# Layer 1's probabilities turned by VectorE's blocks and a way by DRAM, and dequantisation's comparisons as rectified differences on ScalarE

## The chip, the cores and the metric

The kernel runs on one core of one Trainium2 chip. A core has five engines that the text names as the profile does: PE (TensorE, the matrix products; PEld is its weight load), DVE (VectorE), ACT (ScalarE), POOL (GpSimd) and SP (SyncE, which issues most DMAs). Data lies in SBUF (128 partitions), products go to PSUM, and inputs, outputs and scratch lie in DRAM. The metric is the device time of one execution in microseconds.

## The reference

Four pairs of an attention and a feed-forward part (layers 0 to 3) work on `x` of 8 x 128 x 512 and a context of the same shape; each adds its result to `x`, which is normalised in front of it. All of it is fp32. Two places matter here. Layer 1's attention takes each batch's 128 x 512 matrix as four windows of 128 columns, and in each window has 8 heads of 8 channels:

```python
qh = q.reshape(BN, H, dh, W)          # BN = 8 batches x 4 windows, H = 8, dh = 8, W = 128
kh = k.reshape(BN, H, dh, W)
vh = val.reshape(BN, H, dh, W)
scores = jnp.einsum('bhdi,bhdj->bhij', qh, kh) / jnp.sqrt(jnp.asarray(dh, qh.dtype))
scores = jnp.where(mp[:, :, None, :] > 0, scores, jnp.asarray(-1000000000.0, scores.dtype))
attn = jax.nn.softmax(scores, axis=-1)
o = jnp.einsum('bhij,bhdj->bhdi', attn, vh).reshape(BN, DK, W)
```

Layer 2's feed-forward weights are first rounded to 16 levels per block of 64 (NF4), with the block's largest magnitude as its scale:

```python
normalized = flat / jnp.where(absmax == 0, 1.0, absmax)
bounds = (NF4_CODE[:-1] + NF4_CODE[1:]) * 0.5
idx = jnp.searchsorted(bounds, normalized)
return (NF4_CODE[idx] * absmax).reshape(shape)
```

Three matrices of 1376 x 512 go through this.

## The kernel before, in words

**Units.** Layers 0 and 2's attention are 128 units, each one head of 128 channels for four batches ("half"): units 0 to 31 and 32 to 63 are Layer 0's two halves, 64 to 95 and 96 to 127 Layer 2's. A unit projects keys, queries and (per group of four heads) values, makes scores (L265), takes the softmax (reduction L256 and reciprocal L259 on DVE, exponentials L213 on ACT), turns the probabilities, weighs the values (L288), and after each fourth head projects to the output (L218). Step `u` of the main loop projects for unit `u+3`, scores unit `u+2` and weighs unit `u`, so a unit's probabilities have two steps in which to be turned. Turning goes by `turn_far`: DVE transposes 32 x 32 blocks (L277), SP sends the tile to a DRAM scratch `far` and reads it back in four DMAs in which the blocks change places. Only the first three units turn by PE (`turn`).

**Side work.** Between the pieces of a unit the main loop calls `slot()`. A table gives for each slot what else runs there: while Layer 0's second half runs, the table holds Layer 0's feed-forward, Layer 1 and its feed-forward for the first half's four batches (`short_stages`); the same for the second half stands beside Layer 2's first half. The side work has a stream of its own (`side`), with three PSUM buffers for all purposes; the units' stream (`main`) has two for projections and one each for transposes, scores and weighed values.

**Layer 1.** Per batch and window `n`, `score` (slot t+2+3n) makes the 8 heads' scores with two products (L532), adds the mask, takes the softmax over 128 x 8 x 128 in one tile `s` (L534, L536, L213, L539, L540). `turn` (slot t+7+3n) transposes the 8 heads on PE (L225, two groups of four into PSUM) and copies each group to SBUF on ACT (L228). `weigh` (slot t+9+3n) multiplies with the values (L551, 8 products of 32 columns).

**Dequantisation.** The three weight matrices pass in 34 chunks of up to 128 x 512. In each, `nf4_round` takes 15 steps: a comparison of the weights with a bound, times the difference of two levels (L725; the first, L721, writes the sum itself), and an addition to the sum (L726), both on DVE. The steps are generated one at a time, and each `slot()` lets through as many as `NF4_PACE` says for the stage (a pair per half: with the table still filled, and after). Each chunk is then transposed on PE and written to DRAM for Layer 2's feed-forward.

**What sets the order.** The program is recorded as above; a scheduler in the framework then orders each engine's instructions, and each engine runs its own list in order, waiting on semaphores. SP's list holds the weight loads, whose 20 buffers are freed by PE, and the trips by DRAM, in one queue; a DMA that reads what another has written waits on SP for it. Layer 3 follows the units; it makes the same trip by DRAM through its method `far`, at 128 x 768 for queries and keys and 128 x 1024 for probabilities.

Of the kernel before, what the change touches and what calls it, by code (L numbers as in the profile page):

```python
# [62 lines left out]
def kernel(ctx: ExitStack, tc: tile.TileContext, a, out):  # L63
# [157 lines left out]
    def p_transposed(st, p, engine=None):  # L221
# [8 lines left out]
            V.tensor_copy(pt, tp)  # L230
        return pt

    def project(st, w, xT):

        mm = st.mm()
        for c in range(DC):
            T.matmul(mm, lhsT=w[:, c, :], rhs=xT[:, c, :], start=c == 0, stop=c == DC - 1)  # L237
        return mm

    def tile_of(name, bufs, shape=(P, 512)):  # L240
        return qkv.tile(list(shape), F32, tag=name, name=name, bufs=bufs)
# [6 lines left out]
    class Unit:  # L248
# [24 lines left out]
            self.pt = [pt[:, i, :] for i in range(HALF)]  # L273

        def turn_far(self):
            tb = tile_of("tb", 1, (P, 4, HALF, 32))
            V.transpose(tb, self.p.rearrange("p i (c k) -> p c i k", k=32))  # L277
            far = dram.tile([4, 32, 4, P], F32, tag="far0", name="far0", bufs=4)
            load(far.rearrange("a k b n -> (a k) (b n)"), tb.rearrange("p c i j -> p (c i j)"))
            pt = self.st.wide("pt", (P, 4, HALF, 32))  # L280
            for b in range(4):
                load(pt[32 * b:32 * b + 32].rearrange("p a i j -> p a (i j)"), far[:, :, b, :].rearrange("a k n -> k a n"))
            self.pt = [pt[:, :, i, :] for i in range(HALF)]

        def weigh(self):
# [28 lines left out]

    def l0_rms(st, h):

        sq = st.wide("sq", bufs=1)
        ss = st.small(1, "ss")
        S.activation(sq, h, AF.Square, accum_out=ss)
        V.tensor_scalar(ss, ss, 1.0 / D, 1e-5, ALU.mult, ALU.add)  # L320
        done = inv_sqrt(ss, [P, 1])
        r = st.wide("pt", (P, 4, P)).rearrange("p c q -> p (c q)")
        V.tensor_scalar(r, h, ss, None, ALU.mult)
        return r, done

# [144 lines left out]
    class L1:  # L470
        def __init__(self, st, hf):
            self.st, self.hf = st, hf
            self.pools = ExitStack()
            self.l1 = self.pools.enter_context(tc.tile_pool(name="l1", bufs=2))
            l1c = self.pools.enter_context(tc.tile_pool(name="l1c", bufs=1))
            self.wqk = l1c.tile([P, 3, 64], F32, name="wqk")
            load(self.wqk, a["l1_wqkv"])
            self.wo = l1c.tile([P, P], F32, name="wo1")
            G.memset(self.wo, 0.0)
            for h in range(8):  # L480
                r = 32 * (h % 4) + 8 * (h // 4)
# [12 lines left out]
            self.vt = l1c.tile([P, 4, 8, 32], F32, name="vt")  # L494
            G.memset(self.vt, 0.0)
            self.s, self.pts = {}, {}

        def norm(self, b):
            mk = self.l1.tile([P, D], F32, tag="mk", name="mk", bufs=1)
            load(mk, a["mask_ff1"][b].to_broadcast([P, D]))  # L500
            self.neg = self.l1.tile([P, D], BF16, tag="neg", name="neg", bufs=1)
            V.tensor_scalar(self.neg, mk, 0.0, -BIG, ALU.is_le, ALU.mult)
            self.ct = load_ctx(self.st, b)
            self.h = layernorm(self.st, b)
# [20 lines left out]

        def score(self, b, n):
            st, w = self.st, slice(n * P, (n + 1) * P)
            s = self.s[n] = self.l1.tile([P, 8, P], F32, tag="s1", name="s1")
            scs = [st.sc() for j in range(2)]
            for j in range(2):  # L530
                r = slice(32 * j, 32 * (j + 1))
                T.matmul(scs[j], lhsT=self.qk[r, w], rhs=self.km[r, :, w], start=True, stop=True)  # L532
            for j in range(2):
                V.scalar_tensor_tensor(s[:, 4 * j:4 * j + 4, :], scs[j], 1.0 / math.sqrt(8.0), times(self.neg[:, w], 4), ALU.mult, ALU.add)  # L534
            mx = st.small(8, "mx")
            V.tensor_reduce(mx, s, AX.X, ALU.max, negate=True)  # L536
            su = st.small(8, "su8")
            exps(lambda h: s[:, h, :], lambda h: s[:, h, :], su, 8, mx)
            V.reciprocal(su, su)  # L539
            V.tensor_mul(s, s, along(su, P))  # L540

        def turn(self, b, n):
            self.pts[n] = [p_transposed(self.st, self.s[n][:, 4 * j:4 * j + 4, :], S) for j in range(2)]

        def weigh(self, b, n):
            if n == 0:
                self.o = self.l1.tile([P, D], F32, tag="o1", name="o1", bufs=1)
            pv = self.st.pv()
            for j in range(2):
                for i in range(4):  # L550
                    T.matmul(pv[32 * i:32 * i + 32, 0, :], lhsT=self.vt[:, n, 4 * j + i, :], rhs=self.pts[n][j][:, i, :], start=j == 0, stop=j == 1)  # L551
            S.copy(self.o[:, n * P:(n + 1) * P], pv[:, 0, :])

        def close(self, b):
            self.y = self.st.wide("sq", bufs=1)
            load(self.y, a["mask_ff1"][b].to_broadcast([P, D]))
            S.activation(self.o, self.o, AF.Gelu)

# [7 lines left out]
    class F1:  # L566
# [33 lines left out]
        def output(self, b):  # L600
            mm = self.st.mm()
            for c in range(DC):
                T.matmul(mm, lhsT=self.qt[b][:, c, :], rhs=self.wb16[:, c, :], start=c == 0, stop=c == DC - 1)
            y = self.st.wide("sq", bufs=1)
# [109 lines left out]

    def nf4_round(dst, w):

        for i, (cmp, bound, step) in enumerate(NF4_STEPS):
            if i == 0:  # L720
                V.tensor_scalar(dst, w, bound, step, cmp, ALU.mult)  # L721
                continue
            ind = nfp.tile([P, 512], F32, tag="ind", name="ind", bufs=1)
            iv = ind[:w.shape[0], :w.shape[1]]
            V.tensor_scalar(iv, w, bound, step, cmp, ALU.mult)  # L725
            V.tensor_add(dst, dst, iv)  # L726
            yield

    def nf4_scales(ri, am):

# [169 lines left out]
    class L3:  # L900
# [50 lines left out]
            V.tensor_scalar(it.rq, it.rq, P * 1e-6, None, ALU.add)  # L951
            inv_sqrt(it.rq, [P, 4])

        def far(self, src, h, tag):

            n = src.shape[2] // P
            tb = self.l3.tile([P, 4 * n, h, 32], F32, tag="tb" + tag, name="tb3", bufs=1)  # L960
            V.transpose(tb, src.rearrange("p h (c k) -> p c h k", k=32))
            far = dram.tile([4, 32, n, 4, 32 * h], F32, tag="far" + tag, name="far", bufs=4)
            load(far.rearrange("a i s b n -> (a i) (s b n)"), tb.rearrange("p c h j -> p (c h j)"))
            pt = self.l3.tile([P, n, 4, h, 32], F32, tag="pt" + tag, name="pt3", bufs=3)
            for b in range(4):
                load(pt[32 * b:32 * b + 32].rearrange("p s a h j -> p s a (h j)"), far[:, :, :, b, :].rearrange("a i s n -> i s a n"))
            return pt

        def turn(self, it):
            it.t = self.far(it.qk, 6, "qk")[:, 0]  # L970

        def order(self, it):

# [4 lines left out]
            it.kT = t[:, :, 4:6, :].rearrange("p a s j -> p s a j")  # L978

        def turn_near(self, it):  # L980
            t = self.l3.tile([P, 6, P], F32, tag="ptqk", name="pt3", bufs=3)
            for h in range(0, 6, 2):
                tp = self.st.tp()[:, 0:2, :]
                for j in range(2):
# [25 lines left out]
            it.pts = [p_transposed(self.st, it.p[:, :, j * P:(j + 1) * P]) for j in range(2)]  # L1010

        def turn_blocks(self, it):
            pt = self.far(it.p, 4, "p")
            it.pts = [pt[:, j].rearrange("p a h j -> p (a h j)") for j in range(2)]

        def weigh(self, it):
# [76 lines left out]
    with ExitStack() as early:  # L1093
# [3 lines left out]
        ps = sub_pool("ps", 1, space=PSUM)  # L1097
        qkv = sub_pool("qkv", 5)
        nfp = sub_pool("nf4", 2)
        main = Stream("m", sub_pool("main", 2), ps, {"mm": ("mm", 2), "tp": ("tp", 1), "sc": ("sc", 1), "pv": ("pv", 1)})  # L1100
        side = Stream("s", sub_pool("side", 2), ps, {k: ("side", 3) for k in ("mm", "tp", "sc", "pv", "po")})


        NF4_PACE = ((2.1, 2.1), (1.0, 2.2), (0.45, 1.2), (1.2, 1.2))
        xT0, xT2 = [], []


# [49 lines left out]
        def short_stages(hf):  # L1157
# [26 lines left out]
            for i, b in enumerate(batches(hf)):  # L1184
                t = 18 + 13 * i
                for n in range(4):
                    call(t + 7 + 3 * n, "l1", "turn", b, n)
                    call(t + 9 + 3 * n, "l1", "weigh", b, n)
                call(t + 18, "l1", "close", b)
                call(t + 19, "l1", "output", b)  # L1190
# [280 lines left out]
```

## Time and profile before

| what | us |
|---|---|
| median of 3 runs (lowest to highest) | 3104.28 (3103.65 to 3104.73) |
| the profiled execution's own time | 3106.4 |
| its span, first to last instruction | 3104.6 |
| mean granted TensorE clock | 0.998 of full |
| DMA: share of 16 engines' span, queue of SP | 36.6% |
| Layer 1's transposes on PE with the first three units' (L225) | 35.3 busy, 268 instructions |
| their copies on ACT (L228) | 35.8 busy, 67 instructions |
| dequantisation's comparisons on DVE (L725, L721) | 210.5 and, of full size, 13.6 |
| dequantisation's additions on DVE (L726) | 326.8 |

A group's row reads: line, engine, operation, written tile <- read tiles, sizes, count, then busy us and mean ns of one, then the idle time of the engine before it and what ended it. PE shows an fp32 product as two instructions, a transpose as one. Matmuls are pipelined, so the length of one overlaps the next; the distance from start to start is what a product takes of PE.

### The profile page before, as it was taken

What the parts mean: (1) busy time and instruction counts of PE and PEld (TensorE: products, weight loads), DVE (VectorE), ACT (ScalarE), POOL (GpSimd) and SP (SyncE); (2) the same over time, 40 slices, a digit from 0 to 9 for tenths busy, and PEclk for the clock granted to TensorE, in tenths of its full rate; (3) what the DMA queues carried; (4) which work ended last, traced back from release to release, by engine and by line L of the source; (5) the groups of instructions that cost most, each with busy time, mean ns of one, the idle gap of its engine ahead of it and who ended that gap; (6) DMA issues with size and microseconds to landing.
All of it is one profiled execution on the core that took longest, in us unless ns stands there. A gap on an engine that the chain in (4) does not pass through costs nothing.

```text
span 3104.6 us, 34843 instructions
## 1 busy us (share of the span) xinstructions
PE 3071.9 (99%) x10976; PEld 1694.2 (55%) x10980; DVE 2015.8 (65%) x4209; ACT 1086.1 (35%) x3410; POOL 295.5 (10%) x315
## 2 busy tenths in 40 slices
PE   9999999999999999999999999999999999999999
PEld 4554555545554565555555554445665665555564
DVE  5877787667767766888989983113555555555544
ACT  3222222235543233655333332002434433333332
POOL 2000000000001021111111110001111111111110
PEclk9999999999999999999999999999999999999999
DMA  6434343333334432323444342223655655555540
GB/s 216 124 113 126 117 126 116 102 103 97 102 95 118 150 119 80 102 82 113 123 140 128 119 124 84 77 69 103 181 178 165 187 180 174 180 172 167 174 132 14
DMA packets 414807, 393.83 MB, mean 127 GB/s; under 512 B 37600, under 2 KB 312736, under 8 KB 414112
## 3 DMA queue, kind: packets, MB, share of 16 engines
q1 hardware_dynamic: 391200, 348.60, 36.6%
q10 hardware_dynamic: 23040, 41.95, 4.4%
q8 instruction: 89, 1.46, 0.2%
q0 software_dynamic: 384, 1.05, 0.1%
q14 instruction: 94, 0.77, 0.1%
HBM read 291.92 MB, written 99.55 MB: 126 GB/s over the span
## 4 chain that ended last, share of the span: by engine, by line
PE 84%; DVE 11%; ACT 2%; DMA 2%; issue 1%; POOL 0%; SPq 0%; ACTq 0%; POOLq 0%; DVEq 0%
PE mm L237 17%; PE mm L218 12%; PE po L218 7%; PE tp L921 7%; PE mm L376 7%; PE mm L944 7%; PE mm L879 5%; PE pv L1019 4%; PE sc L996 3%; PE pv L288 2%; PE mm L888 2%; PE sc L265 2%; ACT s L213 1%; DVE dq L726 1%; DVE rot L656 1%; PE mm L666 1%
## 5 line engine op out<-in xcount | busy, mean ns | idle before, releaser
L237 PE MATMUL mm<-xT,w 128*128 128x512 f32 x1024 | 464.4, 595 | 2.1 <-DVE rot L656 2.1
L218 PE MATMUL mm<-w,o 128*128 128x512 f32 x1024 | 464.0, 597 | 1.6 <-ACT o L290 1.5
L726 DVE TENSOR_TENSOR dq<-dq,ind 128x512 f32<-128x512 f32 (+2 forms) x476 | 326.8, 687 | 9.8
L237 PEld LDWEIGHTS mm<-xT,w 128*128 128x128 f32 x1024 | 188.9, 190 | 218.6 <-issue 208.6
L218 PEld LDWEIGHTS mm<-w,o 128*128 128x128 f32 x1024 | 188.5, 191 | 214.3 <-issue 199.9
L213 ACT ACTIVATE s<-s,nm 128x128 f32<-128x128 f32 x512 | 199.0, 390 | 190.2 <-DVE nm L256 179.1
L944 PE MATMUL mm<-w,xT 128*128 128x512 f32 x512 | 233.9, 592 | 0.0
L218 PE MATMUL po<-w,o 128*128 128x512 f32 x512 | 233.2, 594 | 0.0
L237 PE MATMUL mm<-ctxT,w 128*128 128x512 f32 x512 | 230.7, 593 | 1.1 <-ACT ctxT L1235 0.8
L376 PE MATMUL mm<-w,ctxT 128*128 128x512 f32 x512 | 230.4, 593 | 0.0
L725 DVE TENSOR_SCALAR ind<-nw 128x512 f32<-128x512 f32 (+2 forms) x476 | 210.5, 442 | 5.8
L213 ACT ACTIVATE p<-sc,nm,rq 128x256 f32<-128x256 f32 x256 | 141.1, 562 | 113.6 <-DVE nm L1001 109.9
L159 POOL TENSOR_TENSOR rs<-rs,mhalf 128x1 f32<-128x1 f32 x64 | 41.2, 645 | 1248.5 <-DVE rs L180 757.7
L265 PEld LDWEIGHTS sc<-k,q 128*128 128x128 f32 x1024 | 131.8, 192 | 49.5 <-issue 39.9
L219 DVE TENSOR_TENSOR x<-x,mm 128x512 f32<-128x512 f32 x128 | 87.0, 679 | 110.3 <-PE mm L218 110.0
L290 ACT COPY o<-pv 128x512 f32<-128x512 f32 x128 | 74.3, 581 | 237.6 <-PE pv L288 237.6
L218 PEld LDWEIGHTS po<-w,o 128*128 128x128 f32 x512 | 96.3, 190 | 110.6 <-issue 103.3
L879 PE MATMUL mm<-xT,w 128*128 128x512 f32 (+1 forms) x352 | 152.5, 592 | 0.8 <-DVE x L219 0.8
L376 PEld LDWEIGHTS mm<-w,ctxT 128*128 128x128 f32 x512 | 94.3, 190 | 106.2 <-issue 106.2
L1000 DVE TENSOR_REDUCE nm<-sc 128x2 f32<-128x512 f32 x128 | 85.3, 674 | 102.7 <-PE sc L996 102.5
L237 PEld LDWEIGHTS mm<-ctxT,w 128*128 128x128 f32 x512 | 93.2, 190 | 99.3 <-issue 96.8
L944 PEld LDWEIGHTS mm<-w,xT 128*128 128x128 f32 x512 | 97.0, 190 | 89.5 <-issue 84.9
(244 smaller groups left out, 4716.5 us busy)
## 6 DMA issues: line engine op xcount, KB each, us to landing
w<-in_l_wq SPq DMA_DIRECT2D x128, 256.0 KB
w<-in_l_wo SPq DMA_DIRECT2D x128, 256.0 KB
far<-tb SPq DMA_DIRECT2D x125, 256.0 KB
pt<-far SPq DMA_DIRECT2D x500, 64.0 KB
far<-tb SPq DMA_DIRECT2D x60, 512.0 KB
pt<-far SPq DMA_DIRECT2D x240, 128.0 KB
far<-tb SPq DMA_DIRECT2D x63, 384.0 KB
pt<-far SPq DMA_DIRECT2D x252, 96.0 KB
```

What stands on the lines that cost most here:

```text
L213: S.activation(dst(h), src(h), AF.Exp, bias=negm[:, h:h + 1], scale=by, accum_out=su[:, h:h + 1])
L218: T.matmul(mm, lhsT=o(h), rhs=wo[h], start=h == 0, stop=h == 3)
L237: T.matmul(mm, lhsT=w[:, c, :], rhs=xT[:, c, :], start=c == 0, stop=c == DC - 1)
L265: T.matmul(sc[:, i, :], lhsT=self.q[:, i * P:(i + 1) * P], rhs=k[:, i * P:(i + 1) * P], start=True, stop=True)
L376: T.matmul(mm, lhsT=ctxT[:, c, toks(self.hf * HALF + i)], rhs=grp.wv[c], start=c == 0, stop=c == DC - 1)
L725: V.tensor_scalar(iv, w, bound, step, cmp, ALU.mult)
L726: V.tensor_add(dst, dst, iv)
L879: T.matmul(mm[:n, :], lhsT=w[c][:, j * P:j * P + n], rhs=xT[:, c, :], start=c == 0, stop=c == DC - 1)
L921: T.matmul(it.kv[:, s, :], lhsT=lhsT, rhs=it.wkv[c // 2][:, c % 2, :], start=c == 0, stop=c == DC - 1)
L944: T.matmul(mq, lhsT=self.xT[it.hf][:, c, cols(it.b)], rhs=it.wq[c], start=c == 0, stop=c == DC - 1)
L996: T.matmul(sc[:, i, :], lhsT=it.qT[2 * j + i], rhs=it.kT, start=True, stop=True)
L1019: T.matmul(pv, lhsT=it.v[:, j, :], rhs=it.pts[j], start=j == 0, stop=j == 1)
```

## The change

- Layer 1's `turn` on PE, its PSUM tiles and its copies are gone. At the end of `score`, the 8 heads' probabilities (128 x 1024) are transposed in blocks on DVE, sent to DRAM and read back in four DMAs by a new function `blocks_turned`, which Layer 0's, Layer 2's and Layer 3's trips now use too, with the same layout as before. `weigh` reads the heads' columns as four runs of 32. The tile `s` has one buffer instead of two.
- `nf4_round` no longer compares. ACT makes `max(0, (w - bound) * 2^100)`, which is 0 below the bound and at least the step above it; DVE then takes the minimum with the step and adds it to the sum in one instruction. Downward bounds have the sign turned, with the neighbouring float as bound. ACT works one step ahead; the difference's tile `ind` has two buffers instead of one. A column of 15 constants `bounds` is set on POOL at the start.
- `NF4_PACE` changes for the second to fourth half.
- Some tiles share buffers: the `main` stream's wide tiles come from the tags `o` and `pt0`, the side stream's `sq` has two buffers and also serves for Layer 1's mask and for the first normalisation's result.

```diff
+    def blocks_turned(pool_, src, name, bufs):
+        h, n = src.shape[1], src.shape[2] // P
+        tb = pool_.tile([P, 4 * n, h, 32], F32, tag="tb" + name, name="tb", bufs=bufs[0])
+        V.transpose(tb, src.rearrange("p h (c k) -> p c h k", k=32))
+        far = dram.tile([4, 32, n, 4, 32 * h], F32, tag="far" + name, name="far", bufs=4)
+        load(far.rearrange("a i s b n -> (a i) (s b n)"), tb.rearrange("p c h j -> p (c h j)"))
+        pt = pool_.tile([P, n, 4, h, 32], F32, tag="pt" + name, name="pt", bufs=bufs[1])
+        for b in range(4):
+            load(pt[32 * b:32 * b + 32].rearrange("p s a h j -> p s a (h j)"), far[:, :, :, b, :].rearrange("a i s n -> i s a n"))
+        return pt
...
         def turn_far(self):
...
+            pt = blocks_turned(qkv, self.p, "0", (1, 2))[:, 0]
             self.pt = [pt[:, :, i, :] for i in range(HALF)]
...
         def score(self, b, n):
-            s = self.s[n] = self.l1.tile([P, 8, P], F32, tag="s1", name="s1")
+            s = self.l1.tile([P, 8, P], F32, tag="s1", name="s1", bufs=1)
...
             V.tensor_mul(s, s, along(su, P))
-
-        def turn(self, b, n):
-            self.pts[n] = [p_transposed(self.st, self.s[n][:, 4 * j:4 * j + 4, :], S) for j in range(2)]
+            self.pts[n] = blocks_turned(self.l1, s, "1", (1, 2))[:, 0]
...
-                    T.matmul(pv[32 * i:32 * i + 32, 0, :], lhsT=self.vt[:, n, 4 * j + i, :], rhs=self.pts[n][j][:, i, :], start=j == 0, stop=j == 1)
+                    T.matmul(pv[32 * i:32 * i + 32, 0, :], lhsT=self.vt[:, n, 4 * j + i, :], rhs=self.pts[n][:, :, 4 * j + i, :], start=j == 0, stop=j == 1)
...
+    HUGE = 2.0 ** 100
+    down = [(float(np.nextafter(np.float32(b), np.float32(2))), -HUGE, -step) for cmp, b, step in NF4_STEPS if cmp == ALU.is_le]
+    up = [(b, HUGE, step) for cmp, b, step in NF4_STEPS if cmp == ALU.is_gt]
+    bounds = keep.tile([P, len(NF4_STEPS)], F32, name="bounds")
+    for i, (b, f, _) in enumerate(down + up):
+        G.memset(bounds[:, i:i + 1], -f * b)
...
     def nf4_round(dst, w):
-        for i, (cmp, bound, step) in enumerate(NF4_STEPS):
+        n = w.shape[0]
+        def past(i):
+            ind = nfp.tile([P, 512], F32, tag="ind", name="ind")[:n, :w.shape[1]]
+            S.activation(ind, w, AF.Relu, bias=bounds[:n, i:i + 1], scale=(down + up)[i][1])
+            return ind
+        then = past(0)
+        for i, (_, _, step) in enumerate(down + up):
+            ind = then
+            if i + 1 < len(NF4_STEPS):
+                then = past(i + 1)
             if i == 0:
-                V.tensor_scalar(dst, w, bound, step, cmp, ALU.mult)
-                continue
-            ind = nfp.tile([P, 512], F32, tag="ind", name="ind", bufs=1)
-            iv = ind[:w.shape[0], :w.shape[1]]
-            V.tensor_scalar(iv, w, bound, step, cmp, ALU.mult)
-            V.tensor_add(dst, dst, iv)
-            yield
+                V.tensor_scalar(dst, ind, step, None, ALU.min)
+            else:
+                V.scalar_tensor_tensor(dst, ind, step, dst, ALU.min, ALU.subtract if i == len(down) else ALU.add)
+                yield
...
-        NF4_PACE = ((2.1, 2.1), (1.0, 2.2), (0.45, 1.2), (1.2, 1.2))
+        NF4_PACE = ((2.1, 2.1), (0.9, 2.2), (0.2, 1.6), (1.6, 1.6))
...
                 for n in range(4):
-                    call(t + 7 + 3 * n, "l1", "turn", b, n)
                     call(t + 9 + 3 * n, "l1", "weigh", b, n)
```

More of the change, by code (lines that the diff above doesn't have):

```diff
@@ L275, in turn_far @@
         def turn_far(self):
[L276 to L282, printed above, removed]
+            pt = blocks_turned(qkv, self.p, "0", (1, 2))[:, 0]
             self.pt = [pt[:, :, i, :] for i in range(HALF)]
@@ L315, in l0_rms @@
     def l0_rms(st, h):
-        sq = st.wide("sq", bufs=1)
+        r = st.wide("sq")
         ss = st.small(1, "ss")
-        S.activation(sq, h, AF.Square, accum_out=ss)
+        S.activation(r, h, AF.Square, accum_out=ss)
         V.tensor_scalar(ss, ss, 1.0 / D, 1e-5, ALU.mult, ALU.add)
         done = inv_sqrt(ss, [P, 1])
-        r = st.wide("pt", (P, 4, P)).rearrange("p c q -> p (c q)")
         V.tensor_scalar(r, h, ss, None, ALU.mult)
@@ L495, in __init__ @@
             G.memset(self.vt, 0.0)
-            self.s, self.pts = {}, {}
+            self.pts = {}
         def norm(self, b):
-            mk = self.l1.tile([P, D], F32, tag="mk", name="mk", bufs=1)
+            mk = self.st.wide("sq")
             load(mk, a["mask_ff1"][b].to_broadcast([P, D]))
@@ L550, in weigh @@
                 for i in range(4):
-                    T.matmul(pv[32 * i:32 * i + 32, 0, :], lhsT=self.vt[:, n, 4 * j + i, :], rhs=self.pts[n][j][:, i, :], start=j == 0, stop=j == 1)
+                    T.matmul(pv[32 * i:32 * i + 32, 0, :], lhsT=self.vt[:, n, 4 * j + i, :], rhs=self.pts[n][:, :, 4 * j + i, :], start=j == 0, stop=j == 1)
             S.copy(self.o[:, n * P:(n + 1) * P], pv[:, 0, :])
         def close(self, b):
-            self.y = self.st.wide("sq", bufs=1)
+            self.y = self.st.wide("sq")
             load(self.y, a["mask_ff1"][b].to_broadcast([P, D]))
@@ L603, in output @@
                 T.matmul(mm, lhsT=self.qt[b][:, c, :], rhs=self.wb16[:, c, :], start=c == 0, stop=c == DC - 1)
-            y = self.st.wide("sq", bufs=1)
+            y = self.st.wide("sq")
             V.tensor_mul(y, mm, self.wsc)
@@ L952, in queries @@
             inv_sqrt(it.rq, [P, 4])
[L954 to L967, printed above, removed]
         def turn(self, it):
-            it.t = self.far(it.qk, 6, "qk")[:, 0]
+            it.t = blocks_turned(self.l3, it.qk, "qk", (1, 3))[:, 0]
         def order(self, it):
@@ L980, in turn_near @@
         def turn_near(self, it):
-            t = self.l3.tile([P, 6, P], F32, tag="ptqk", name="pt3", bufs=3)
+            t = self.l3.tile([P, 6, P], F32, tag="ptqk", name="pt", bufs=3)
             for h in range(0, 6, 2):
@@ L1012, in turn_blocks @@
         def turn_blocks(self, it):
-            pt = self.far(it.p, 4, "p")
+            pt = blocks_turned(self.l3, it.p, "p", (1, 3))
             it.pts = [pt[:, j].rearrange("p a h j -> p (a h j)") for j in range(2)]
@@ L1099, with wide @@
         nfp = sub_pool("nf4", 2)
-        main = Stream("m", sub_pool("main", 2), ps, {"mm": ("mm", 2), "tp": ("tp", 1), "sc": ("sc", 1), "pv": ("pv", 1)})
+        class Main(Stream):
+            def wide(self, tag, shape=(P, 512), bufs=2):
+                return tile_of(*(("pt0", 2) if tag == "pt" else ("o", 6)), shape)
+        main = Main("m", None, ps, {"mm": ("mm", 2), "tp": ("tp", 1), "sc": ("sc", 1), "pv": ("pv", 1)})
         side = Stream("s", sub_pool("side", 2), ps, {k: ("side", 3) for k in ("mm", "tp", "sc", "pv", "po")})
-        NF4_PACE = ((2.1, 2.1), (1.0, 2.2), (0.45, 1.2), (1.2, 1.2))
+        NF4_PACE = ((2.1, 2.1), (0.9, 2.2), (0.2, 1.6), (1.6, 1.6))
         xT0, xT2 = [], []
```

## The prediction

> **What bounds the kernel now.** I read the page's first part, then the table of stretches, the waits of TensorE (PE), the groups by shape, and last the timeline where Layer 1 runs.
>
> ```profile
> PE 3071.9 (99%) x10976; PEld 1694.2 (55%) x10980; DVE 2015.8 (65%) x4209; ACT 1086.1 (35%) x3410; POOL 295.5 (10%) x315
> ```
>
> PE is busy in all but 32.7 of 3104.6 us; no other engine passes 65%. A mean hides stages, so the stretches come next (columns: PE, weight loads, DVE, ACT, POOL, clock, DMA share, GB/s).
>
> ```profile
> 400.00:500.00 100.00, 100.00 (x302) 49.74 (x301) 79.60 (x161) 22.79 (x67) 0.00 (x0) 1.00 0.40 118
> ...
> 1300.00:1400.00 100.00, 96.20 (x485) 53.28 (x484) 82.77 (x142) 58.96 (x229) 10.92 (x9) 0.98 0.27 83
> ...
> 1700.00:1800.00 100.00, 99.36 (x411) 58.66 (x409) 94.40 (x166) 35.17 (x129) 15.53 (x11) 1.00 0.40 124
> ```
>
> The first row is plain Layer 0, the second has Layer 1 at the side, the third is Layer 2's second half: DVE reaches 94% there, and still PE loses 0.64 us in 100. So PE's own work sets the time in every stage, and what leaves PE is saved unless a new wait takes its place. The waits that exist near the change are small:
>
> ```profile
> PE sc L532 <- ACT pt L228: 1.4, 2, 1.2
> ...
> PE tp L225 <- DVE s L534: 0.6, 1, 0.6
> ```
>
> The rows from which I take prices:
>
> ```profile
> L225 PE MATMUL tp<-ident,s 128*128 128x128 f32 x268 | 35.3, 274 | 0.6 <-DVE s L534 0.6
> L228 ACT COPY pt<-tp 128x512 f32<-128x512 f32 x67 | 35.8, 582 | 18.0 <-PE tp L225 18.0
> L726 DVE TENSOR_TENSOR dq<-dq,ind 128x512 f32<-128x512 f32 x420 | 297.7, 709 | 8.5
> L961 DVE STREAM_TRANSPOSE tb<-p 128x1024 f32<-128x1024 f32 x60 | 74.2, 1237 | 9.5 <-DMA far<-tb 9.5
> L691 DVE SCALAR_TENSOR_TENSOR s<-sc,neg 128x512 f32<-128x512 f32 x64 | 43.6, 682 | 1.3 <-PE sc L265 0.2
> L725 DVE TENSOR_SCALAR ind<-nw 128x512 f32<-128x512 f32 x420 | 189.6, 451 | 5.0
> L319 ACT ACTIVATE sq<-h 128x512 f32<-128x512 f32 x8 | 5.0, 630 | 9.7 <-DVE h L183 7.4 <-DVE rs L180 2.2
> ```
>
> And PE's timeline in Layer 1 (start, length, instructions):
>
> ```profile
> 1305.03 0.64 PE L551 MATMUL pv<-pt,vt 128*32 128x128 f32 x16
> 1305.60 4.54 PE L218 MATMUL mm<-w,o 128*128 128x512 f32 x6
> 1309.98 1.04 PE L225 MATMUL tp<-ident,s 128*128 128x128 f32 x8
> 1310.85 3.60 PE L218 MATMUL mm<-w,o 128*128 128x512 f32 x8
> ```
>
> Eight transposes start at 1309.98 and the next product at 1310.85: they hold PE's stream for 0.87 us with no gap before or behind.
>
> **The change, part by part.**
>
> *PE.* Layer 1 has 2 halves x 4 batches x 4 windows = 32 bundles of 8 transposes (256 of the 268 in L225's row; 12 belong to the first three units and stay). Start to start a bundle holds PE 0.87 us, at 1309.98 and again at 1327.61 and 1336.50: 32 x 0.87 = 27.8 us. The row's busy time gives 35.3 x 256/268 = 33.7 us, but it counts each bundle's drain (1.04 against 0.87), which the next product overlaps. I take 27.8 and keep 33.7 as the other end. The order of the built kernel confirms that 256 transposes go and no product is added. The weighing products (L551) read the same sizes in runs of 32; L288 already reads its `pt` that way behind the trip of its units, at 1.06 us for 8 at 1299.97 and the same with unbroken rows at 58.94, so the stride costs nothing. The waits on the copies (1.4) and for the transposes' source (0.6) go with them: 2.0 us.
>
> *ACT.* 64 copies of 0.582 us leave (37.2 us). 510 rectifications come: 480 of 512 columns, 30 of 192. Between L319 (0.630, a square from SBUF) and L510 (0.687, with a bias, from PSUM), and about 0.4 for the narrow ones, they cost 314 to 342 us. ACT goes from 1086 to some 1377 us, 44%. The built order has 19 table loads on ACT before and after, so no table is added.
>
> The Trainium skill speaks against this move: "ScalarE: Activation LUTs", section Rules for kernel authors, wants relu on VectorE, and gives an activation with a bias per partition as 280 ns + 0.833 ns per element. By that, as an estimate, a rectification is 0.71 us and all of them some 353 us, ACT 45%; the trace agrees that DVE's comparison is shorter (0.451 us), and the sum is the same since neither engine sets the end.
>
> *DVE.* 476 comparisons (L725, its three shapes 189.6 + 11.7 + 9.2) go: 210.5 us. The addition (0.709) becomes a fused minimum and addition; L691, the same form, took 0.682, so nothing is counted. 32 block transposes of 128x1024 come, 1.237 each by L961's row: 39.6 us. DVE falls to about 1845 us, 59%. This is off PE's path; if DVE were binding it would be worth 171 us, which the 99% excludes.
>
> *The trip.* Each bundle now issues one 512 KB DMA out and four of 128 KB in on SP, 160 in all. Layer 3 makes the same trip 60 times. Its SP rows:
>
> ```profile
> 2405.54 0.81 SPq L113 DMA_DIRECT2D far<-tb  x2
> 2409.20 5.84 SPq L113 DMA_DIRECT2D pt<-far  x8
> ```
>
> Each row holds two trips, of 512 and of 384 KB. The way out takes 3.7 us until SP goes on, the four issues 1.7 to 2.9; the landing of the last I put at 2 to 3.7, bounded by the way out. That makes 7.4 to 10.3 us. In Layer 1 the products of a score end at 1305.1 and L540 at 1313.8, so softmax is 8.7 us; with the transpose 1.24 and the trip, the probabilities are ready 17.3 to 20.2 us after the score. The cover is PE's other work: in the changed order, priced by rows (0.86 us per 512-column product, 0.22 per 128, 0.11 per transpose), 22.1 us lie between a score and its weighing in the tightest bundle, 23.4 in the next, and 28 or more in 24 of the 32. Not late by these numbers, so 0; every us beyond stalls PE directly. Behind the waiting SP stand weight loads and the units' own trips. Weights come from 20 buffers, and SP waits for PE to free them (L121 <- PE mm L237, 326.8 us in 122 waits), so they are several units ahead.
>
> *The units' softmax.* This cover is thinner. At 1730.53 Layer 2's score starts, its transposed copies are issued at 1741.83, the last at about 1743.6, and weighing starts at 1747.44: some 2 us spare after landing. In the new order one or two rectifications stand between the exponentials and the scaling (L694) on ACT, up to 1.3 us, and each needs DVE to have freed one of two `ind` tiles; DVE has one comparison of 0.43 less at two places of the same chain. Net -0.9 to +1.3; I take 0. If uncovered: half of the 32 units of the last stage are that tight, so 16 x 1.3 = 21 us.
>
> *The pace.* The new rates move dequantisation out of Layer 1's second run: between units 64 and 95, 44 steps instead of 57, and 124 instead of 103 afterwards; both orders finish before the last four units, so nothing is left to drain alone.
>
> *Start.* 15 memsets of a column stand before the identity on POOL. At 0.10 each at most they end by 3 us; PE's first transpose starts at 6.21. No cost, at most 1.5.
>
> **Sum.** On the profiled execution's span 3104.6 - 27.8 - 2.0 = 3074.8. That execution's own time was 3106.4, 2.1 above the runs' median 3104.28; taking the same 29.8 from the median gives 3074.5, and I write 3075.
>
> **Rivals.**
>
> *Lock-step of ACT and DVE.* The rectification waits for DVE to free a tile, and DVE waits for the rectification; the units' softmax stands in both queues. For it: DVE's 94% at 1700 and the 2 us spare. Against it: DVE loses more work than it gets there. It gives 3075 + 21 = 3096.
>
> *The trip is late (slower).* SP is one queue: a trip of Layer 1 can stand behind a unit's trip that waits for its own transpose (L113 <- DVE tb L277, up to 9.4 us). Summed over the changed order's distances, a readiness of 28 us costs PE 23 us, of 28.5 about 28, of 30 costs 46. So from some 28.5 us the change loses, and at 30 it ends at 3075 + 46 = 3121. For it: those waits sum to 332.9 us over 108. Against it: the chain is 17 to 20 us, and a 9.4 us wait would have to fall on most bundles. The Trainium skill, "VectorE: DVE Perf Modes", section Rules for kernel authors, tells to transpose 128x128 on TensorE where PSUM may take it, and calls a rearranging plain DMA a trap (section The three transpose paths). The trace disagrees for this layout: with 60 such trips Layer 3's stretch 2200 to 3000 has PE at 100.00 in each 100 us.
>
> *The transposes were no cost.* If they filled time in which PE would wait anyway (3.8 us of idle in 1300 to 1400), the time stays at 3104. Against it: of those gaps only the 2.0 us named touch the transposes, and work stands ready behind each bundle.
>
> **Chances.** Forecast 0.77, lock-step 0.13, late trip 0.07, no cost 0.03. A measurement of this kernel tells 0.2%, 6 us, from no change. 3096 is 0.27% faster, so of the lock-step case 0.10 counts as faster, 0.02 as same and 0.01 as slower: faster 0.87, same 0.05, slower 0.08. The forecast's own range is 3066 to 3084: down by the other price of the transposes (5.9) and some idle that DVE's relief gives back (3 of the 11.9 us in 1130 to 1500), up by half the lock-step's price. Up to the lock-step case whole: 3066 to 3096 for 8 in 10.
>
> **What would show it.** Right: L225 falls to 12 and PE's busy time to about 3042; PE's idle stays at 30 to 34 us; weighing of Layer 1 waits for no DMA; DVE near 1845, ACT near 1377. Wrong: PE waits at the weighing of Layer 1 for `pt` (late trip), at the units' weighing or at evictions by ACT or DVE (lock-step), or PE's busy time falls while its idle grows by as much (no cost).

## The result, and the profile after

The changed kernel takes 3081.09 us (median of 4 runs, 3077.42 to 3083.17), against 3104.51 us (4 runs, 3103.65 to 3108.34) for the kernel before on the same chip. The ratio is 0.9921, with a 95% interval of 0.9904 to 0.9938: 23.4 us less, where 29.5 were forecast. The profiled execution took 3082.39 us, and its span is 3080.6.

The page's first part, after:

```profile
PE 3043.1 (99%) x10720; PEld 1668.2 (54%) x10724; DVE 1878.8 (61%) x3765; ACT 1373.5 (45%) x3856; POOL 294.0 (10%) x330
```

PE has 256 instructions and 28.8 us of busy time less than before. Its idle time, though, is now 3080.6 - 3043.1 = 37.5 us, against 32.7. So not all that left PE was saved. The same three stretches as before (PE, weight loads, DVE, ACT, POOL, clock, DMA share, GB/s) say where:

```profile
400.00:500.00 100.00, 100.00 (x302) 49.77 (x302) 63.20 (x117) 54.10 (x115) 0.00 (x0) 1.00 0.39 118
1300.00:1400.00 100.00, 90.94 (x444) 48.05 (x435) 81.40 (x129) 55.33 (x213) 11.71 (x9) 0.97 0.62 169
1700.00:1800.00 100.00, 98.83 (x405) 58.35 (x404) 84.29 (x144) 63.45 (x182) 15.06 (x11) 1.00 0.41 128
```

DVE is relieved in the first and the third, as it should be, and PE is as full there as before to about half a us. In the second, where Layer 1 runs beside Layer 2's first half, PE loses 9.1 us instead of 3.8, and the granted clock is 0.97. The waits of PE (what waited, for what: total us, times, longest) name the cause:

```profile
PE tp L654 <- issue: 5.3, 1, 5.3
PE mm L672 <- DMA w<-in_l_wkv: 4.9, 1, 4.9
PE tp L190 <- DMA h<-in_ctx: 2.8, 1, 2.8
PE mm L252 <- DMA w<-in_l_wq: 2.7, 1, 2.7
```

The first and the third have counterparts in the kernel before, of 4.1 us (L648) and 2.3 us (L190). The second and the fourth are new: PE waits for *weights*, of which the list of the kernel before has none. PE's timeline (start, length, then idle time before in brackets) shows the price of the two waits:

```profile
1353.84 5.37 PE L672 MATMUL mm<-ctxT,w 128*128 128x512 f32 x8 [4.89 <-DMA w<-in_l_wkv]
1359.05 3.73 PE L682 MATMUL mm<-w,ctxT 128*128 128x128 f32 x32
1362.62 1.06 PE L297 MATMUL pv<-pt,v 128*128 128x128 f32 x8
1363.51 1.02 PE L516 MATMUL mm<-h,wqk 128*128 128x512 f32 x2
1367.27 5.40 PE L252 MATMUL mm<-xT,w 128*128 128x512 f32 x8 [2.73 <-DMA w<-in_l_wq]
```

Eight instructions of this size, which is four fp32 products, took 3.60 us in the kernel before, where the same line stands so:

```profile
1374.59 3.60 PE L666 MATMUL mm<-ctxT,w 128*128 128x512 f32 x8
```

Behind the two stalls they take 5.37 and 5.40. From 1350 to 1370 the granted clock is 0.85. So the two stalls cost 4.9 + 2.7 us of idle time and 1.8 + 1.8 us of slow products, 11.2 us in all.

Why the weights came late stands in the timeline of SP, the queue that issues them. First the kernel before, the two loads that feed the same line's products at 1374.59:

```profile
1289.12 0.33 SPq L121 DMA_DIRECT2D w<-in_l_wkv  x1
...
1298.45 0.38 SPq L121 DMA_DIRECT2D w<-in_l_wkv  x1
```

Then the changed kernel, up to the loads for the products at 1353.84:

```profile
1307.82 8.92 SPq L113 DMA_DIRECT2D far<-tb  x2
1316.79 0.92 SPq L121 DMA_DIRECT2D w<-in_l_wo  x2
1317.82 3.86 SPq L113 DMA_DIRECT2D pt<-far  x8
1322.17 8.24 SPq L113 DMA_DIRECT2D far<-tb  x2
...
1347.62 2.79 SPq L113 DMA_DIRECT2D far<-tb  x2
1350.46 0.92 SPq L121 DMA_DIRECT2D w<-in_l_wkv  x2
```

Before, the loads were issued 76 and 85 us ahead of their use; after, 3.4 us ahead of the moment at which PE could start, and PE had stood for 4.9 us by then. Between the weight loads stand the trips, Layer 1's and the units' own, a way out (`far<-tb`) or its reads (`pt<-far`) in most rows, and rows of two ways out that last 8 to 9 us because SP waits within them (an issue alone takes 0.33).

The groups by shape (busy us, mean ns | idle before and its causes) hold the rest of the change:

```profile
L739 ACT ACTIVATE ind<-nw,bounds 128x512 f32<-128x512 f32 x450 | 316.2, 718 | 218.1 <-DVE dq L750 149.4 <-issue 36.8 <-DVE nw L837 11.3
...
L750 DVE SCALAR_TENSOR_TENSOR dq<-ind,dq 128x512 f32<-128x512 f32 x420 | 300.7, 716 | 20.6 <-ACT ind L739 7.1
...
L240 DVE STREAM_TRANSPOSE tb<-s 128x1024 f32<-128x1024 f32 x32 | 39.6, 1239 | 0.4
```

And among PE's own groups, Layer 1's weighing and what is left of the transposes:

```profile
L557 PE MATMUL pv<-pt,vt 128*32 128x128 f32 x512 | 20.6, 279 | 0.2 <-issue 0.2
...
L225 PE MATMUL tp<-ident,s 128*128 128x128 f32 x12 | 1.8, 275 | 0.0
```

The transposes are down to the 12 of the first units. Layer 1's weighing (L557) waited for no DMA: the probabilities themselves are in time, and what came late is what stands behind them in SP's queue.

### The profile page after: what moved, and what is told of

Same layout as the page of the kernel before. It is cut to its first block, busy times and chain, and to the rows that moved or that the text cites. A ratio compares the mean times of both kernels' runs of the same rounds, so it can differ in the third digit from the quotient of the medians.

```text
span 3080.6 us, 35006 instructions
## 1 busy us (share of the span) xinstructions
PE 3043.1 (99%) x10720; PEld 1668.2 (54%) x10724; DVE 1878.8 (61%) x3765; ACT 1373.5 (45%) x3856; POOL 294.0 (10%) x330
## 4 chain that ended last, share of the span: by engine, by line
PE 47%; DVE 3%; ACT 1%; issue 0%; POOL 0%; DVEq 0%; ACTq 0%; POOLq 0%
PE po L218 7%; PE tp L945 7%; PE mm L968 7%; PE mm L903 5%; PE pv L1028 4%; PE mm L218 4%; PE sc L1005 3%; PE mm L252 3%; PE mm L912 2%; PE mm L1096 1%; PE mm L1084 1%; PE pv L297 1%; DVE dq L750 1%; PE sc L280 1%; PE mm L682 1%; PE mm L672 1%
## 5 line engine op out<-in xcount | busy, mean ns | idle before, releaser
L739 ACT ACTIVATE ind<-nw,bounds 128x512 f32<-128x512 f32 (+2 forms) x510 | 350.0, 703 | 238.7 <-DVE dq L750 164.3
L750 DVE SCALAR_TENSOR_TENSOR dq<-ind,dq 128x512 f32<-128x512 f32 (+2 forms) x476 | 333.7, 701 | 22.9 <-ACT ind L739 8.0
L213 ACT ACTIVATE s<-s,nm 128x128 f32<-128x128 f32 x512 | 198.3, 388 | 102.6 <-DVE nm L271 101.6
L213 ACT ACTIVATE p<-sc,nm,rq 128x256 f32<-128x256 f32 x256 | 141.2, 563 | 113.9 <-DVE nm L1010 110.2
L384 PEld LDWEIGHTS mm<-w,ctxT 128*128 128x128 f32 x512 | 94.6, 190 | 107.6 <-issue 106.6
```

Of the source, the lines that this page charges most:

```text
L213: S.activation(dst(h), src(h), AF.Exp, bias=negm[:, h:h + 1], scale=by, accum_out=su[:, h:h + 1])
L384: T.matmul(mm, lhsT=ctxT[:, c, toks(self.hf * HALF + i)], rhs=grp.wv[c], start=c == 0, stop=c == DC - 1)
L739: S.activation(ind, w, AF.Relu, bias=bounds[:n, i:i + 1], scale=(down + up)[i][1])
L750: V.scalar_tensor_tensor(dst, ind, step, dst, ALU.min, ALU.subtract if i == len(down) else ALU.add)
```

## The experiments

Each time is a median, with the lowest and highest run, and each ratio is to runs of the kernel before on the same chip. Differences between two experiments are of such medians, in part from different chips; the kernel before took 3104.17 to 3106.28 us on them, and the interval of most ratios is some 5 us to either side. My theory was that the trip costs PE by SP's queue; its rivals were the time of the trip itself, the added block transposes on DVE, the rectifications on ACT, and the pace.

**The transposes alone** (the kernel before, edited). Layer 1's transposes and copies are left out, and the values are weighed with probabilities that are not turned.

```diff
-            self.pts[n] = [p_transposed(self.st, self.s[n][:, 4 * j:4 * j + 4, :], S) for j in range(2)]
+            self.pts[n] = [self.s[n][:, 4 * j:4 * j + 4, :] for j in range(2)]
```

> The kernel before, with Layer 1's 256 transposes and 64 copies left out: the probabilities are weighed as they stand, untransposed. Nothing is put in their place. Both theories: the bare price of the transposes on PE, 27.8 us start to start and 2.0 us of waits, so some 3075 us. By the busy time (33.7 us) it would be 3069. If the transposes filled time in which PE waits anyway, 3104.

Measured: 3074.83 us (3072.17 to 3075.90), ratio 0.9901 (0.9885 to 0.9918), 29.9 us less. This is the gain that there was to have, and the forecast's 29.8 was right for it. PE's busy time falls by 29.4 us (3071.9 to 3042.5).

**The trip without the rectification** (the changed kernel with the old `nf4_round` and the old `NF4_PACE`).

```diff
-            S.activation(ind, w, AF.Relu, bias=bounds[:n, i:i + 1], scale=(down + up)[i][1])
+            V.tensor_scalar(iv, w, bound, step, cmp, ALU.mult)
...
-                V.scalar_tensor_tensor(dst, ind, step, dst, ALU.min, ALU.subtract if i == len(down) else ALU.add)
+            V.tensor_add(dst, dst, iv)
```

> The changed kernel with the old comparisons on VectorE and the old pace: Layer 1's trip by DRAM alone. Theory A (weight loads stand behind the trips in SP's queue and come late): PE again waits for weights in Layer 1's second run, 5 to 12 us, so 3080 to 3087. Theory B (ACT and DVE in lock-step cost the missing 6 us): no late weights, some 3075.

Measured: 3094.49 us (3091.67 to 3096.73), ratio 0.9965 (0.9952 to 0.9977). This is above both ranges. Only 10.2 us of the 29.9 are left, so the trip gives back 19.7 us here. PE's waits in this kernel:

```profile
PE mm L672 <- DMA w<-in_l_wkv: 4.8, 1, 4.8
...
PE sc L540 <- DVE km L521: 3.2, 2, 1.7
```

The late weights are there without any rectification, and so are waits for DVE in Layer 1's scores.

**The rectification without the trip** (the changed kernel with Layer 1's `turn` on PE and the old pace; the two buffers of `s`, the call of `turn` and the reading in `weigh` go back with it).

```diff
-            self.pts[n] = blocks_turned(self.l1, s, "1", (1, 2))[:, 0]
+            self.s[n] = s
...
+        def turn(self, b, n):
+            self.pts[n] = [p_transposed(self.st, self.s[n][:, 4 * j:4 * j + 4, :], S) for j in range(2)]
```

> The changed kernel with Layer 1 turned on PE as before and the old pace: the rectified differences on ScalarE alone. Theory A: PE loses and gains nothing, 3101 to 3107. Theory B: 3108 to 3112, with PE waits at evictions and at the units' weighing.

Measured: 3099.87 us (10 runs, 3097.76 to 3101.41), ratio 0.9983 (0.9974 to 0.9993). It is 4.9 us faster than the kernel before, below both ranges, with 319 us more of work on ACT and 178 less on DVE; PE's idle falls from 32.7 to 28.9 us. A lock-step of ACT and DVE would have shown here. DVE's waits for the rectified tile in this kernel:

```profile
DVE dq L751 <- ACT ind L742: 11.8, 14, 0.9
...
DVE dq L753 <- ACT ind L742: 7.4, 25, 0.7
```

Nineteen us in a whole execution, none over 0.9: DVE almost always finds its tile ready, and ACT is the one that waits (`ind L742 <- DVE dq L753`, 161.8 us in 127 waits). The kernel also has the change's new sharing of tile buffers, which no run tests alone, so the 4.9 us are those of both.

**Both ways of the trip on POOL's queue** (the changed kernel; only Layer 1's five DMAs per bundle change their issuer).

```diff
-        load(far.rearrange("a i s b n -> (a i) (s b n)"), tb.rearrange("p c h j -> p (c h j)"))
+        send(far.rearrange("a i s b n -> (a i) (s b n)"), tb.rearrange("p c h j -> p (c h j)"))
...
-            load(pt[32 * b:32 * b + 32].rearrange("p s a h j -> p s a (h j)"), far[:, :, :, b, :].rearrange("a i s n -> i s a n"))
+            send(pt[32 * b:32 * b + 32].rearrange("p s a h j -> p s a (h j)"), far[:, :, :, b, :].rearrange("a i s n -> i s a n"))
...
-            self.pts[n] = blocks_turned(self.l1, s, "1", (1, 2))[:, 0]
+            self.pts[n] = blocks_turned(self.l1, s, "1", (1, 2), G)[:, 0]
```

`send` issues on the queue of the engine that is named last, here `G` for POOL.

> The changed kernel with Layer 1's five transfers per bundle issued from POOL's queue, so that SP's weight loads do not stand behind them. Theory A: no wait for weights in Layer 1's second run, 8 to 11 us less than the changed kernel: 3070 to 3073, unless POOL's own waits hold up the rotary additions. Theory B: the same as the changed kernel, 3081.

Measured: 3074.61 us (3073.06 to 3074.99), ratio 0.9904 (0.9887 to 0.9920): 6.5 us less than the changed kernel, at the same work, and 1.6 above the range for this theory. No wait for weights is left among PE's, and the `w<-in_l_wkv` loads are issued 68 and 76 us ahead of their use again.

**Both ways on POOL, with the old comparisons and pace.** This is the second experiment with the fourth's edit.

> Layer 1's trip alone (old comparisons on VectorE, old pace), with its five transfers issued from POOL's queue. Theory A (what the trip costs is that SP's weight loads stand behind it): close to the kernel without the transposes, 3075 to 3081. Theory C (the traffic itself, or the block transposes on a busy VectorE, cost it): as the trip alone from SP, 3092 to 3096.

Measured: 3084.93 us (3082.28 to 3090.41), ratio 0.9940 (0.9923 to 0.9956). It lies between the two ranges, so neither theory is the whole. Of the 19.7 us that the trip cost with the old comparisons, SP's queue is 9.6 (3094.49 - 3084.93). The other 10.1 us (to 3074.83) stay without late weights. The stretch of Layer 1's second run, 1130 to 1500, first in this kernel:

```profile
1130.00:1500.00 370.00, 352.99 (x1631) 197.96 (x1632) 321.75 (x580) 171.85 (x657) 101.48 (x129) 0.99 0.49 146
```

And in the kernel with both ways on POOL and the rectification:

```profile
1130.00:1500.00 370.00, 358.56 (x1662) 202.13 (x1663) 304.75 (x536) 194.19 (x706) 101.80 (x130) 0.99 0.49 148
```

DVE is busy 321.75 of 370 us in the first and 304.75 in the second, and PE loses 5.6 us more in the first. PE's largest wait there is for Layer 1's masked keys on DVE (`sc L541 <- DVE km L522`, 4.9 us in 3 waits), against 1.3 in the second. I read this as the block transposes being dear where DVE is fuller, with the rectification making room for them. That is not shown: the two kernels also differ in the pace and in ACT's work, and 10.1 against 5.6 us differ by no more than the intervals. That the two halves of the change help each other is clearer with the trip on SP: it alone gained 10.2 us and the rectification alone 4.9, and both together 23.4.

**The old pace** (the changed kernel).

```diff
-        NF4_PACE = ((2.1, 2.1), (0.9, 2.2), (0.2, 1.6), (1.6, 1.6))
+        NF4_PACE = ((2.1, 2.1), (1.0, 2.2), (0.45, 1.2), (1.2, 1.2))
```

> The changed kernel with the old pace of dequantisation: 0.45 steps per slot beside Layer 1's second run instead of 0.2, 1.2 instead of 1.6 after it. Theory A: every step of VectorE beside Layer 1 delays the block transposes that SP's queue waits for, so weights come later: 3083 to 3088. If the pace is nothing but a place for the steps: 3081.

Measured: 3083.40 us (3078.43 to 3086.43), ratio 0.9932 (0.9916 to 0.9949). The changed kernel's runs (3077.42 to 3083.17) overlap with this spread, so the pace's share, 2.3 us by the medians, is not told from nothing.

**Sixteen weight buffers, before and after.** If a lead of the loads is what is lost, a shorter lead should cost only the changed kernel.

```diff
-    wpool = pool("wpool", 20)
+    wpool = pool("wpool", 16)
```

> The kernel before with 16 weight buffers instead of 20: SP's loads run one unit less ahead. Theory A: before, the loads have lead to spare, so 3104 to 3108.

> The changed kernel with 16 weight buffers instead of 20. Theory A: the loads have no lead to spare beside Layer 1's second run, so more waits for weights there, 3090 to 3105, and the gain over the kernel before with 16 buffers is less than 15 us. Theory C: the same step as the kernel before with 16 buffers.

Measured: before 3105.25 us (10 runs, 3103.57 to 3109.33), ratio 1.0002 (0.9992 to 1.0011); after 3088.28 us (3084.61 to 3090.40), ratio 0.9943 (0.9927 to 0.9960). Four buffers less cost the kernel before nothing and the changed one 7.2 us. PE's waits in the latter:

```profile
PE mm L252 <- DMA w<-in_l_wq: 4.7, 2, 3.0
...
PE mm L218 <- DVE rot L662: 3.3, 1, 3.3
PE mm L672 <- DMA w<-in_l_wkv: 2.8, 1, 2.8
```

The kernel before had buffers to spare, and the changed one has none. But the loss is not longer waits for weights: they are 7.5 us here and 7.6 in the changed kernel. What is new is the wait for DVE's rotary step (3.3), and how fewer weight buffers lead to it is not shown. The changed kernel loses less than expected, too, and the gain over the kernel before with 16 buffers is 17.0 us, not less than 15.

**No turning at all, with the rectification and the new pace.** As in the first experiment, the values are weighed with probabilities that are not turned; `s` has two buffers again, as in the kernel before.

```diff
-            self.pts[n] = blocks_turned(self.l1, s, "1", (1, 2))[:, 0]
...
+            self.pts[n] = [self.s[n][:, 4 * j:4 * j + 4, :] for j in range(2)]
```

> Both halves of the change without the trip: no transposes and no copies in Layer 1 (the probabilities are weighed untransposed, nothing in their place), rectified differences on ScalarE, new pace. If the parts add up: 3104.5 - 29.9 - 4.9 = 3070. Then the trip costs 11 us from SP's queue and 4 to 5 from POOL's with this dequantisation. If the gain of the rectified differences only existed beside Layer 1's old turn, 3074 to 3076, and the trip from POOL costs nothing.

Measured: 3069.02 us (3068.09 to 3074.16), ratio 0.9891 (0.9876 to 0.9907). The parts add: 3104.7 - 29.9 - 4.9 = 3069.9. Against this floor the trip costs 12.1 us from SP (3081.09) and 5.6 from POOL (3074.61).

**Both ways on POOL, with less dequantisation beside Layer 1.**

```diff
-        NF4_PACE = ((2.1, 2.1), (0.9, 2.2), (0.2, 1.6), (1.6, 1.6))
+        NF4_PACE = ((2.4, 2.4), (0.9, 2.4), (0.0, 1.6), (1.6, 1.6))
```

> The changed kernel with Layer 1's trip from POOL and a pace that leaves no step of dequantisation beside Layer 1's second run (0.0), and more in Layer 0 (2.4). Theory A with VectorE as the second cause: waits for its evictions beside Layer 1's second run shrink, 3068 to 3073. If VectorE has room there already: as the trip from POOL, 3074 to 3075.

Measured: 3076.93 us (5 runs, 3075.81 to 3078.28), ratio 0.9913 (0.9900 to 0.9927). A miss: 2.3 us more than with the changed kernel's pace, where 1.6 to 6.6 us less, or no change, were expected. PE's waits are spread thinly, 3.6 us for the units' scaled scores among them (`sc L281 <- DVE s L698`). The remaining 5.6 us of the trip are not won back by moving the steps in this way.

**Both ways on ACT's queue.** The edit is the fourth's, with `S` for `G`.

> The changed kernel with Layer 1's transfers issued from ScalarE's queue instead of SP's. Theory A: weights on time as with POOL, but ScalarE's exponentials and evictions stand behind each wait for a block transpose or for the way out (about 2 us, 32 times, part of it in PE's path): 3075 to 3090. Theory C (the traffic): 3081.

Measured: 3138.06 us (3133.80 to 3139.91), ratio 1.0105 (1.0090 to 1.0121): 57 us more than from SP and slower than the kernel before, where 3075 to 3090 were expected. The page's engines, and two of ACT's waits:

```profile
PE 3075.5 (98%) x10721; PEld 1682.2 (54%) x10724; DVE 1887.0 (60%) x3765; ACT 1371.1 (44%) x3856; POOL 295.2 (9%) x330
```

```profile
ACT s L213 <- DMA pt<-far: 30.7, 7, 6.3
...
ACT s L213 <- DVE tb L241: 7.2, 4, 4.1
```

ACT has as much work as in the changed kernel. But the exponentials (L213, the units' and Layer 1's) now stand behind the trip's issues in ACT's queue. Some of their waits end with DVE's transpose (7.2 us), more with the reads' own issues (30.7), as here:

```profile
884.66 5.47 ACTq L246 DMA_DIRECT2D pt<-far  x4
890.24 0.40 ACT L213 ACTIVATE s<-s,mx 128x128 f32<-128x128 f32 x1 [6.33 <-DMA pt<-far]
```

Four reads take 1.75 us on SP in the kernel before; why they take up to 7.93 on ACT (at 712.17), the trace does not say. None of these waits of L213 existed with the trip on SP. What they delay is spread over scores, evictions and PE: PE is idle for 61.4 us of the span, 23.9 more than in the changed kernel, and the same count of products holds PE 32.4 us longer, at a mean clock of 0.991 against 0.998 (0.96 from 1130 to 1500).

**Only the reads on POOL.** The way out stays on SP. The edit is shown against the fourth's. This asks which of SP's two new kinds of wait takes the lead away.

```diff
-        send(far.rearrange("a i s b n -> (a i) (s b n)"), tb.rearrange("p c h j -> p (c h j)"))
+        load(far.rearrange("a i s b n -> (a i) (s b n)"), tb.rearrange("p c h j -> p (c h j)"))
```

> The changed kernel with Layer 1's way out to DRAM still on SP and only the four reads back issued from POOL. This tells which of SP's two kinds of new waits uses up the lead of the weight loads. If it is the wait of the way out for the block transpose (tb, 107.7 us in the stretch 1130 to 1500 of the changed kernel, 69.1 with both ways on POOL), SP still stands there 32 times, PE waits for w in Layer 1's second run again by 2 us or more, and the time stays at 3078 to 3083. If it is the wait of the reads for the way out (far), the waits for w vanish and the time is 3073 to 3077, as with both ways on POOL (3074.6).

Measured: 3074.06 us (3072.66 to 3074.99), beside 3106.28 (7 runs, 3105.26 to 3107.36) for the kernel before, ratio 0.9896 (0.9879 to 0.9912). As good as with both ways on POOL. SP's timeline, the two loads for the products that start at 1346.63 with no wait:

```profile
1271.54 0.33 SPq L121 DMA_DIRECT2D w<-in_l_wkv  x1
...
1280.39 0.38 SPq L121 DMA_DIRECT2D w<-in_l_wkv  x1
```

The lead is back, 66 to 75 us, though SP still waits for a transpose's tile 28 times in 1130 to 1500, for 75.1 us. So the way out may stay on SP; the reads may not. In that stretch SP issues 164 reads of `pt<-far` in the changed kernel, whose timeline rows sum to 82.3 us; here it is 107 in 47.4 us, and in the kernel before 103 in 46.8. That is 35 us of SP's time. Where SP's 370 us go, by the sums of its waits:

| SP, 1130 to 1500, us | before | changed | only the reads on POOL |
|---|---|---|---|
| waits for PE to free a weight buffer (L121), its spare time | 107.6 | 58.0 | 108.9 |
| waits for a transpose's tile (L113 <- DVE tb) | 82.3 | 107.7 | 75.1 |
| waits for a way out to land (L113 <- DMA far<-tb) | 31.8 | 15.9 | 44.1 |
| other waits | 41.7 | 43.9 | 33.7 |
| the rest of the 370, SP at its issues | 106.6 | 144.5 | 108.2 |

Of the 49.6 us of spare time that are lost, 37.9 are more time at issues and 9.5 more waits for the trips' two kinds of data together (114.1 to 123.6). With the reads on POOL those waits are still 119.2 us, and the spare time is back. So the time met the expectation for the reads' waits, but by this account it is mostly their issuing, and not their waiting, that used up the lead: the changed kernel waits the least of the three for a way out to land. It is an account and no proof, since a wait is put down to what ended it last, and the scheduler also places SP's instructions anew.

The Trainium skill, "Trainium Kernel Development and Optimization", section Key Constraints, says that issuing DMAs from several engines saves only the sequencer's issue time. The trace agrees as far as the data goes: the stretch moves 146 GB/s with the reads on SP and 150 with them on POOL. But taking the reads' issues off SP is worth 7 us here, because the weights stand in the same queue. That the stretch moves no less data in that run also speaks against the traffic as the cause of these 7 us.

## Why the prediction was right, and where it was mis-sized

**What was right.** The time fell inside the range, on the forecast's side of every rival. The step that carries it, 32 bundles at 0.87 us and 2.0 us of waits, gave 29.8 us, and the run without the transposes measured 29.9. The distance from start to start thus fits better as the price than the rows' busy time (33.7), by which the time would have been near 3069, below all four runs; the interval alone does not exclude it. L225 fell to 12. PE's first transpose starts at 6.22 us, against 6.21: the memsets cost nothing. The weighing of Layer 1 waits for no DMA on PE, as the cover of 22 us against a chain of 17 to 20 said.

**What was luck.** The total came out because two terms that the sum put at nothing have opposite signs: without the 4.9 us of the rectification, the 12.1 us of the trip would have led to 3086, outside the forecast's own range. PE's busy time, about 3042 by forecast and 3043.1, holds 3.6 us of slowed products. ACT's, 1377 by forecast and 1373.5, comes of longer rectifications (350.0 us) whose records overlap: its rows sum to 314.1 us more than before, its busy time to 287.4 more. And one of the prediction's own signs failed: PE's idle time, which was to stay at 30 to 34 us, is 37.5.

**The step that failed.** "Weights come from 20 buffers, and SP waits for PE to free them (L121 <- PE mm L237, 326.8 us in 122 waits), so they are several units ahead." With that, the trip was priced at 0. It measured 12.1 us from SP. The sentence was true of the kernel before at the place shown, with a lead of 76 to 85 us. But SP's waits for PE are the spare time that makes the lead, and the trip was not charged to them. The sum over the kernel hid this too: the 326.8 us are spread over all the stages, and where Layer 1 runs for the second time all of SP's waits for PE (L121) come to 107.6 us. Into this stretch the change puts 61 more reads and 16 more ways out. The numbers for it were in the prediction: four issues at 1.7 to 2.9 us for each bundle. For the 16 bundles of one run of Layer 1 that is 27 to 46 us, and the rows showed 35. They were added to the latency of the probabilities only, and not to the queue.

**The smaller part of the trip.** Even with its reads on POOL the trip costs 5.0 to 5.6 us. With the old comparisons it is 10.1, at a busier DVE. What these are made of stays open. Candidates are the 39.6 us of block transposes, which the prediction called off PE's path, and the added traffic; no run tests either alone. PE's waits there are single ones of 1 to 2.5 us at several lines, and the attempt with the pace failed. Some are for the trips by DRAM: the units' weighing waits for `pt<-far` for 2.4 us with both ways on POOL and 2.0 with the reads there, Layer 1's for 0.3 and 1.5. The lists of the kernel before and of the kernel without any turning have no such wait.

**The rectification** was taken at no gain and was worth 4.9 us. The forecast's own range held "some idle that DVE's relief gives back (3 of the 11.9 us in 1130 to 1500)", which is this term in kind, but it was kept out of the sum. By the profile the rectification alone saves 3.8 us of PE's idle time, of which 1.6 are in that stretch and 1.7 in 1500 to 2100. Its instruction took 0.718 us, above the prediction's rows of 0.630 and 0.687, and all of them 350.0 against 314 to 342. The Trainium skill, "ScalarE: Activation LUTs", section What ACT_TABLE_LOAD costs, states 280 ns + 0.833 ns per element for a bias per partition, by which, as an estimate, this size takes 0.71 us; the trace agrees with that. Its preference for VectorE (section Rules for kernel authors) did not hold here: moved to ScalarE, which has time, the longer instruction (0.718 against 0.451 us) came out 4.9 us cheaper.

**DVE** is at 1878.8 instead of 1845 us. The rows changed as forecast (476 comparisons out, 32 transposes at 1.239 in, additions 333.7 against 326.8). But an engine's busy time is less than the sum of its rows, as the records of neighbours overlap: DVE's rows sum to 2164.0 us before and 2005.6 after, which is 158.4 less, and its busy time falls by 137.0. So taking the rows' times out of the busy time took too much.

**The rivals.** Lock-step did not occur: DVE waited 13.0 and 8.0 us in all for rectified tiles in the changed kernel, and the rectification alone made the kernel faster. "No cost" fell with the first experiment. The late trip had the right place, SP's one queue, but the wrong victim: the prediction named the weight loads behind the trip, but priced only what the *trip* would wait for there. The warning of the Trainium skill that it cites against this trip ("VectorE: DVE Perf Modes", section The three transpose paths) is for a large innermost stride at the destination; the reads here write whole runs of 32 columns per head, so Layer 3's rows neither bear it out nor speak against it.

**The sum, repaired:** 3104.5 - 29.9 (transposes) - 4.9 (rectification) + 12.1 (trip from SP) = 3081.8, against 3081.1 measured. The 12.1 is itself taken from the changed kernel and the kernel without turning, so the check on the sum is the latter alone: 3069.9 by the parts, 3069.0 measured.

## What to carry to other kernels

When DMAs are added to a queue, charge their issue time and their waits to that queue in the stage where they fall, and compare this with the queue's spare time (its waits for free buffers) in that same stage; a prefetch that is "far ahead" on average can be at the end of its lead there. DMAs that come in number and must wait for their data belong on a queue that carries nothing urgent: here the reads on POOL gave 7 us, while both ways on ACT's queue cost 57. Where an engine is to take on new work, try it together with what relieves it: with both ways on POOL, the trip cost 10.1 us beside the old comparisons and 5.6 beside the rectification.

## What the runs showed of the hardware that was not expected

- A stall of PE costs more than its length. Behind waits of 4.89 and 2.73 us, eight instructions took 5.37 and 5.40 us instead of 3.60, and the granted clock was 0.85 over those 20 us. The Trainium skill, "TensorE: Matmul & The Clock Gate", section "Part 1: The HAM clock gate", halves the clock after an idle window of about 3.4 us, and for as long again once work is back; by that, as an estimate, work behind a stall takes 1.7 us longer. The trace agrees with the size (1.8 and 1.8 us). It agrees with the threshold for the first stall only: the second is shorter, and began 10.7 us after the first had ended. With the trip on ACT, a wait of 2.19 us was followed by eight instructions in 5.21 us, too. Nor is the threshold borne out in the kernel before, where a wait of 1.04 us was followed by six instructions in 4.54 us (1305.60 in the prediction's lines) and a clock of 0.72 from 1305 to 1311; six of the same line took 2.84 behind a wait of 0.90 us. So the length of a wait alone does not tell its price here:

```profile
1303.98 1.12 PE L532 MATMUL sc<-km,qk 32*128 32x512 f32 x2 [1.04 <-DVE vt L521]
...
1332.19 1.13 PE L532 MATMUL sc<-km,qk 32*128 32x512 f32 x4 [0.90 <-DVE km L513]
...
1333.82 2.84 PE L218 MATMUL mm<-w,o 128*128 128x512 f32 x6
```

- With that, many short waits can be dear: from 1130 to 1500 the kernel with the trip on ACT had a granted clock of 0.96, against 0.99 in the changed kernel.
